# Local attention layers: outputs ahead of the query turn, MLP steps and output products one tile earlier

## The chip, the cores and the metric

The kernel runs on one core of one Trainium2 chip. The metric is device time in microseconds of one execution; the runs below are executions of the same program. The engines are named as in the profile: PE (TensorE, with PEld for its weight loads), DVE (VectorE), ACT (ScalarE), POOL (GpSimd) and SP (SyncE, whose queue issues most DMAs).

## The reference

The whole program is two adaptive layer-norm blocks over x of 4 x 1024 x 128 in float32. Block 0 is a linear attention and a mixture of experts. Block 1 is a windowed attention and, as its second half, two **local layers**. Only the local layers are touched. Cut to what matters, with 8 heads of 64 and a window of 64:

```python
def layer(x, wqkv, qs, ksc, wo, lg, lb, w1, b1, w2, b2):
    h = shift_token(x)                        # second half of the features from one token before
    q, k, v = split_heads(h @ wqkv)
    q, k = rotary_xpos(l2norm(q) * qs, l2norm(k) * ksc)
    sim = 8.0 * q @ look_around(k).T          # own window of 64 tokens and the one before, masked
    o = softmax(sim) @ look_around(v)
    x = x + merge_heads(o) @ wo
    h = layernorm(shift_token(x)) * lg + lb
    a, g = split(h @ w1 + b1)                 # 341 wide each
    return x + (a * gelu(g)) @ w2 + b2
```

## The kernel before

One function, `adaln_blocks`, builds the whole program. PE runs its instructions in the order in which the calls are written (its part is under a manual schedule). The order on DVE, ACT, POOL and SP is worked out when the program is built, by a planner that starts from the written order and lets an instruction that it takes to be ready go ahead of one that it takes to wait; a few calls are pinned with `issue_after`. Every engine then runs its own list strictly in order and waits on semaphores.

The local layers start at about 571 us. They work on tiles of 128 tokens: 8 tiles (`NT`) to a batch row, 4 rows (`B`), 2 layers (`DEPTH`), so 64 tiles. One loop over g, from -1 to 67, is a software pipeline. In round g it does, for the tiles that exist:

- `scores(g)`: 16 products of query and key (`s`, L958, 64 x 64 pieces of the array), and behind them on DVE eight masked sums with running minimum (`pr<-s`, L968, which also give `mx`).
- `project(g + 3, 0)` and `(g + 3, 1)`: the query and the key product (`qk`, L658). ACT squares each (`sq`, L661). DVE makes `co` (L663), `si` (L668) and the sum of squares `ss` (L670), in this order; `co` waits for the square. POOL adds `co` and `si` (L678), takes the power of `ss` (L674) and scales the keys (L680).
- `turn(g + 2, 0)`: four transposes of the query (`qktr`, L894), copied by ACT to `qT` (L901). For tiles 3 to 7 of the first row `co` and `si` are turned separately and added in PSUM (L898).
- `flip(g - 2, 0)` and `(g - 2, 1)`: transposes of the weights (`ptr`, L1002), copied by ACT to `pt` (L1004).
- `over_sums(g - 1)`: reciprocal (L988) and the scaling of the weights, half on POOL and half on DVE (L995); in the first row's later tiles ACT takes DVE's half (L993).
- `exps(g)`: eight exponentials on ACT (L980).
- `outputs(g - 3)`: 16 products of values and weights (`o`, L1016, 128 x 64 pieces), copied by ACT to `os` (L1020).
- `turn_keys(g + 2)`: DVE transposes the keys in blocks (`tk`, L921); SP writes them to DRAM (`kd`) and reads them back (`kT`), which `scores` needs two rounds later.
- `values(g - 1)`: the value product (`v`, L938), ACT's copy `vs` (L940) and two DMAs on SP (`ve`).
- every fourth round `project_out` (`yp`, L1027), which DVE adds to the residual (L1028).
- the side steps of a batch row, one half of 512 tokens at a time, from a table `steps`: `mlp_in` (transposes L1048, then statistics on DVE and POOL), `mlp_out` (transposes L160, ACT's `hn` L161), `mlp_gate` (L1062, then gelu on ACT, L1066, between two table loads, since exp and gelu need different tables), `mlp_up` (L1071, DVE L1073), `mlp_down` (L1079, DVE L1080) and, in the last layer, `write` (transposes L1089, ACT's copy L1091 and a DMA on SP).

All PE results but the scores go through one ring of six PSUM buffers (`pM`, tag `mid`); a new one can be written when the engines have read the one six allocations earlier. The scores have two buffers of their own (`pS`). The last batch row of the last layer has its own list of steps at the end (`parts`).

The written order of one round before was: scores, project 0, (early query turn), flip 0, over_sums, project 1, flip 1, exps, (late query turn), outputs, turn_keys, first side step, values, project_out, other side steps. The query turn stood early only in rounds 1 to 5:

```python
            if 0 < g < NT - 2:
                when(g + 2, turn, 0)
```

Of the kernel before, what the change touches and what calls it, by code (L numbers as in the profile page):

```python
# [27 lines left out]
B, N, D = 4, 1024, 128  # L28
NT = N // P
BLK = 512  # L30
# [18 lines left out]
def adaln_blocks(ctx: ExitStack, tc: tile.TileContext, a: dict, out: bass.AP):  # L49
# [637 lines left out]
    EARLY = 3  # L687
# [3 lines left out]
    with (  # L691
# [95 lines left out]
        def project_out(b, k):  # L787
            s = slice(k * BLK, (k + 1) * BLK)
            yp = ps.tile([P, BLK], F32, tag="m", name=f"y1_{b}_{k}")
            pe.matmul(yp, lhsT=wout1, rhs=kept1[b, k, "os"], start=True, stop=True)  # L790
            dve.scalar_tensor_tensor(xT[b][:, s], yp, mods[1][:, 2, b : b + 1], xT[b][:, s], ALU.mult, ALU.add)
# [23 lines left out]
        def when(g, f, *args):  # L815
            if 0 <= g < NG8:
                f(*divmod(g, NT), *args)
# [27 lines left out]
        for g in range(-1, NG8 + 2):  # L845
            b, t = divmod(g, NT)
# [30 lines left out]
    with (  # L877
# [219 lines left out]
        def at(g, f, *args):  # L1097
            steps.setdefault(g, []).append((f, args))
# [5 lines left out]
        for l in range(DEPTH):  # L1104
            for b in range(B):
                g = (l * B + b) * NT
                if (l, b) not in hs:
                    at(g - 5, shift, l, b)
                if l == DEPTH - 1 and b == last:
                    continue  # L1110
                for k, f, after in (
                    (0, mlp_in, 9), (0, mlp_out, 11), (0, mlp_gate, 12), (0, mlp_up, 13), (1, mlp_in, 13), (0, mlp_down, 14),
                    (1, mlp_out, 15), (1, mlp_gate, 16), (1, mlp_up, 17), (1, mlp_down, 18),
                ):
                    at(g + after, f, l, b, k * BLK, (k + 1) * BLK)
                if l == DEPTH - 1:
                    at(g + 16, write, l, b, 0, BLK)
                    at(g + 19, write, l, b, BLK, N)
        tiles = DEPTH * B * NT

        parts = ((0, BLK), (BLK, BLK + 2 * P), (BLK + 2 * P, N))
# [18 lines left out]
        for g in range(-1, tiles + 4):  # L1140
            side = steps.get(g, [])
            when(g, scores)
            when(g + 3, project_mid, 0)

            turns = {-1: (0, 1), 0: (2,)}.get(g, (g + 2,))
            if 0 < g < NT - 2:
                when(g + 2, turn, 0)
            when(g - 2, flip, 0)
            when(g - 1, over_sums)
            when(g + 3, project_mid, 1)  # L1150
            when(g - 2, flip, 1)
            when(g, exps)
            for i in turns:
                if not 0 < g < NT - 2:
                    when(i, turn, 0)
                if i < EARLY and g < EARLY:
                    when(i, turn, 1)
            when(g - 3, outputs)
            if g > 0:
                when(g + 2, turn_keys)  # L1160
            for f, args in side[:1]:
                f(*args)

            for i in {0: (), 1: (0,)}.get(g, (g - 1,)):
                when(i, values)

            f0 = g - 7
            if f0 % 4 == 0 and 0 <= f0 < tiles - NT:
                lo = f0 % NT * P
                project_out(f0 // (B * NT), f0 // NT % B, lo, lo + BLK)  # L1170
            for f, args in side[1:]:
                f(*args)
# [127 lines left out]
```

## Time and profile before

| | us |
|---|---|
| median of 3 runs | 1219.28 (1216.90 to 1220.04) |
| the profiled execution | 1217.85 |
| its span | 1216.0 |
| PE busy | 1117.8 |
| DVE busy | 893.6 |
| ACT busy | 799.8 |
| POOL busy | 797.0 |
| stretch 560 to 1216 (local layers), PE / DVE / ACT / POOL busy | 629.23 / 579.40 / 511.33 / 551.31 |

The span is what the profile covers; the execution's time has a little more around it. Times in views of the profile count from the start of the span. In a timeline a row gives start, duration, engine, line, operation, the tiles written and read, and in brackets the idle time of the engine just before and what ended it. Rows overlap where an engine is pipelined, so the distance from start to start says what an instruction costs in a row of others. PE's granted clock is 1.00 in almost the whole stretch.

### The profile page before, as it was taken

Reading aid. Unit: us, or ns where it says so; the run is one execution under the profiler, and the core shown is the slowest. Engines: PE = TensorE matmul, PEld = TensorE weight load, DVE = VectorE, ACT = ScalarE, POOL = GpSimd, SP = SyncE. Lnnn points to the kernel's source line nnn. Section 1 sums busy time; section 2 is a strip of 40 time slices with the busy share of each in tenths; the row PEclk is TensorE's granted clock in tenths of the full one; section 3 lists DMA queues with packets and bytes.
Section 4 is the critical chain, followed back from the end, with each engine's and each line's share of the span. In section 5 each row is a group of like instructions: output and inputs, shape, how many; then the busy total and the mean of one; then the engine's idle time right before and its main releaser. Section 6 shows DMA issues by size and latency. Waiting matters only on the chain.

```text
span 1216.0 us, 33934 instructions
## 1 busy us (share of the span) xinstructions
PE 1117.8 (92%) x13142; PEld 677.8 (56%) x13142; DVE 893.6 (73%) x2702; ACT 799.8 (66%) x2189; POOL 797.0 (66%) x712
## 2 busy tenths in 40 slices
PE   6789998999888999978899999999999999999998
PEld 5544453444366666655665555555655556555564
DVE  5557273442475577756989999999999999999854
ACT  3353372232476677755798877878878888788772
POOL 4536454747422062516899999899998999888821
PEclk9799999999999899989999999999999999999999
DMA  6030403022132132210234333343333333333320
GB/s 183 1 125 17 140 1 119 23 66 75 28 91 74 53 101 73 68 44 23 75 114 115 100 101 92 88 111 112 106 93 87 106 109 105 110 94 99 104 59 26
DMA packets 111700, 100.68 MB, mean 83 GB/s; under 512 B 9482, under 2 KB 84788, under 8 KB 111540
## 3 DMA queue, kind: packets, MB, share of 16 engines
q1 hardware_dynamic: 111108, 98.00, 27.9%
q8 instruction: 103, 1.69, 0.6%
q10 hardware_dynamic: 432, 0.53, 0.1%
q14 instruction: 57, 0.47, 0.1%
HBM read 57.71 MB, written 20.86 MB: 65 GB/s over the span
## 4 chain that ended last, share of the span: by engine, by line
PE 43%; DVE 26%; ACT 16%; issue 6%; POOL 6%; DMA 2%; SPq 2%; POOLq 0%; ACTq 0%
PE h L496 5%; DVE pr L968 4%; ACT pr L980 4%; PE ptr L751 3%; PE qk L658 3%; DVE si L668 3%; DVE ss L670 3%; DVE tk L921 2%; DVE co L663 2%; PE yp L1027 2%; PE s L958 2%; PE s L269 2%; PE obank L768 2%; PE y L510 2%; PE gm L1062 2%
## 5 line engine op out<-in xcount | busy, mean ns | idle before, releaser
L980 ACT ACTIVATE pr<-pr,mx 128x128 f32<-128x128 f32 x512 | 200.5, 403 | 51.2 <-DVE mx L968 50.5
L678 POOL TENSOR_TENSOR co<-co,si 128x512 f32<-128x512 f32 x123 | 157.7, 1285 | 68.7 <-DVE si L668 67.4
L674 POOL TENSOR_TENSOR ss<-ss,nhalf 128x16 f32<-128x16 f32 x64 | 194.6, 3041 | 5.2
L968 DVE CUSTOM_DVE_ANT_0 pr<-s,masks,ss 128x128 f32<-128x128 f32 x512 | 144.2, 345 | 12.9 <-PE s L958 12.9
L658 PE MATMUL qk<-wqkv,hs 128*128 128x512 f32 x256 | 140.4, 631 | 4.5 <-ACT pt L753 4.5
L500 POOL TENSOR_TENSOR u<-u,cw 128x512 f32<-128x512 f32 x64 | 82.0, 1283 | 81.7 <-ACT u L498 81.7
L496 PE MATMUL h<-hT,w 128*128 128x512 f32 x256 | 122.9, 603 | 6.0 <-DVE g L502 6.0
L502 DVE TENSOR_TENSOR g<-u,h 128x512 f32<-128x512 f32 x64 | 43.9, 686 | 109.1 <-POOL u L500 109.1
L498 ACT ACTIVATE u<-h 128x512 f32<-128x512 f32 x64 | 38.2, 597 | 123.2 <-PE h L496 113.9
L663 DVE TENSOR_TENSOR co<-qk,ab 128x512 f32<-128x512 f32 x128 | 86.6, 676 | 36.1 <-ACT sq L661 36.1
L290 DVE TENSOR_REDUCE mx<-s 128x8 f32<-128x896 f32 x64 | 66.8, 1086 | 51.8 <-PE s L279 51.8
L661 ACT ACTIVATE sq<-qk 128x512 f32<-128x512 f32 x128 | 75.3, 588 | 44.4 <-PE qk L658 44.1
L980 ACT ACTIVATION_READ_ACCUMULATOR pr<-pr,mx 128x1 f32 x512 | 102.1, 199 | 0.0
L1002 PEld LDWEIGHTS ptr<-ident,pr 128*128 128x128 f32 x512 | 63.4, 141 | 63.4 <-issue 50.9
L995 POOL TENSOR_TENSOR pr<-pr,sm 128x512 f32<-128x512 f32 x64 | 78.7, 1229 | 14.2 <-DVE sm L988 7.9
L668 DVE TENSOR_TENSOR si<-qk,ab 128x512 f32<-128x512 f32 x128 | 87.1, 681 | 0.0
L496 PEld LDWEIGHTS h<-hT,w 128*128 128x128 f32 x256 | 47.7, 193 | 69.9 <-issue 50.5
L670 DVE TENSOR_REDUCE ss<-sq 128x8 f32<-128x512 f32 x128 | 86.4, 675 | 0.0
L958 PEld LDWEIGHTS s<-kT,qT 64*64 64x64 f32 x2048 | 56.4, 134 | 43.6 <-issue 24.3
L958 PE MATMUL s<-kT,qT 64*64 64x128 f32 x2048 | 72.3, 278 | 7.1 <-DMA kT<-kd 6.4
L1002 PE MATMUL ptr<-ident,pr 128*128 128x128 f32 x512 | 76.4, 273 | 0.8 <-POOL pr L995 0.7
L753 ACT COPY pt<-ptr 112x512 f32<-112x512 f32 x128 | 71.6, 612 | 8.1 <-PE ptr L751 8.0
(217 smaller groups left out, 2747.9 us busy)
## 6 DMA issues: line engine op xcount, KB each, us to landing
kT<-kd SPq DMA_DIRECT2D x53, 384.0 KB, 3.5
cw<-cd SPq DMA_DIRECT2D x128, 128.0 KB, 3.0
kd<-tk SPq DMA_DIRECT2D x61, 256.0 KB, 2.4
ve<-vs SPq DMA_DIRECT2D x120, 128.0 KB, 2.3
vb<-dv SPq DMA_DIRECT2D x32, 216.0 KB, 2.8
hs<-hT SPq DMA_DIRECT2D x16, 256.0 KB, 3.8
dv<-vt SPq DMA_DIRECT2D x32, 72.0 KB, 1.6
kT<-kd SPq DMA_DIRECT2D x8, 256.0 KB, 2.7
```

The costliest lines, as they stand in the source:

```text
L496: pe.matmul(hh[:, i], lhsT=w[:, c * P : (c + 1) * P], rhs=hT[b][:, blk(k)], start=True, stop=True)
L500: pool.tensor_tensor(u, u, kept[b, k, "cw"][:, c, :], ALU.mult)
L658: pe.matmul(ps, lhsT=hs[l, b][:, t * P : (t + 1) * P], rhs=wl[l][0][:, w, :], start=True, stop=True)
L663: dve.tensor_tensor(co, ph, abs_[l][:, 0, t, w, :].unsqueeze(1).to_broadcast([P, HEADS, DH]), ALU.mult)
L668: dve.tensor_tensor(si.rearrange("p h (i e) -> p h i e", i=2), ex, sn, ALU.mult)
L670: late["summed"] = dve.tensor_reduce(ss[:, w, :], sq, AX.X, ALU.add)
L674: pool.tensor_tensor(ss, ss, nhalf[:, 0:2].unsqueeze(2).to_broadcast([P, 2, HEADS]), ALU.pow)
L678: pool.tensor_tensor(co, co, si, ALU.add)
L958: pe.matmul(S[j][qs, c, :].rearrange("p (g i) -> p g i", i=32), lhsT=q[rw, c, qs], rhs=k[rw, 2 * e : 2 * e + 4, c, :], start=True, stop=True,)
L968: dve.tensor_tensor_reduce(out=pr[:, c, :], in0=S[j][:, c, :], in1=mk[:, min(t, 1), :], scale=kept[l, b, t, "ss"][:, 0, h : h + 1], scalar ...
L980: act.activation(pr[:, c, :], pr[:, c, :], AF.Exp, bias=mx[:, j, c : c + 1], scale=-1.0, accum_out=sm[:, j, c : c + 1])
L1002: pe.transpose(tp[:, c, :], pr[:, c, :], ident)
```

## The change

Four edits in the loop of the local layers:

1. `outputs(g - 3)` stands directly behind `scores(g)`, no longer behind `exps(g)`.
2. The query turn of tile g + 2 stands behind the outputs and ahead of the first projection in all rounds with g > 0. Rounds -1 and 0 keep theirs at the old, late place.
3. All MLP steps and the writes from the table `steps` come one round earlier. The list `parts` of the last row is unchanged.
4. `project_out` comes one round earlier (g - 6 instead of g - 7).

```diff
                 for k, f, after in (
-                    (0, mlp_in, 9), (0, mlp_out, 11), (0, mlp_gate, 12), (0, mlp_up, 13), (1, mlp_in, 13), (0, mlp_down, 14),
-                    (1, mlp_out, 15), (1, mlp_gate, 16), (1, mlp_up, 17), (1, mlp_down, 18),
+                    (0, mlp_in, 8), (0, mlp_out, 10), (0, mlp_gate, 11), (0, mlp_up, 12), (1, mlp_in, 12), (0, mlp_down, 13),
+                    (1, mlp_out, 14), (1, mlp_gate, 15), (1, mlp_up, 16), (1, mlp_down, 17),
                 ):
                     at(g + after, f, l, b, k * BLK, (k + 1) * BLK)
                 if l == DEPTH - 1:
-                    at(g + 16, write, l, b, 0, BLK)
-                    at(g + 19, write, l, b, BLK, N)
+                    at(g + 15, write, l, b, 0, BLK)
+                    at(g + 18, write, l, b, BLK, N)
...
             when(g, scores)
+            when(g - 3, outputs)
+            if g > 0:
+                when(g + 2, turn, 0)
             when(g + 3, project_mid, 0)
-
-            turns = {-1: (0, 1), 0: (2,)}.get(g, (g + 2,))
-            if 0 < g < NT - 2:
-                when(g + 2, turn, 0)
             when(g - 2, flip, 0)
             when(g - 1, over_sums)
             when(g + 3, project_mid, 1)
             when(g - 2, flip, 1)
             when(g, exps)
-            for i in turns:
-                if not 0 < g < NT - 2:
-                    when(i, turn, 0)
-                if i < EARLY and g < EARLY:
-                    when(i, turn, 1)
-            when(g - 3, outputs)
+            for i in {-1: (0, 1), 0: (2,)}.get(g, ()):
+                when(i, turn, 0)
+                when(i, turn, 1)
             if g > 0:
                 when(g + 2, turn_keys)
...
-            f0 = g - 7
+            f0 = g - 6
             if f0 % 4 == 0 and 0 <= f0 < tiles - NT:
```

## The prediction

> **What bounds the kernel now.** I read the page first, then the waits, the busy time by stretches, and last the timelines of VectorE (DVE) and ScalarE (ACT) in one stretch. The page:
>
> ```profile
> PE 1117.8 (92%) x13142; PEld 677.8 (56%) x13142; DVE 893.6 (73%) x2702; ACT 799.8 (66%) x2189; POOL 797.0 (66%) x712
> PE 43%; DVE 26%; ACT 16%; issue 6%; POOL 6%; DMA 2%; SPq 2%; POOLq 0%; ACTq 0%
> ```
>
> PE looks like the bound, but the chain goes through three engines. The edit touches only the local layers, from 571 us to the end. There PE starts `s L958` once a round, and from g = 12 (671.24 us) to g = 60 (1137.92 us) the rounds repeat in fours: a gate round (`gm L1062`), an up round (`a L1071`, then `in_m L1048`), a down round (`ym L1079`) and a product round (`out_m L160`, `yp L1027`). Three such fours, s to s of the gate rounds:
>
> ```profile
> 866.72:905.06 38.34, 37.88 (x367) 22.36 (x366) 35.95 (x120) 31.32 (x98) 35.35 (x29) 1.00 0.40 108
> 905.06:943.37 38.31, 37.89 (x368) 22.36 (x367) 35.76 (x119) 31.34 (x98) 35.07 (x28) 1.00 0.32 93
> 943.37:981.76 38.39, 37.88 (x367) 22.33 (x367) 35.97 (x121) 31.33 (x98) 35.39 (x29) 1.00 0.40 108
> ```
>
> The columns are time, then busy PE, PEld, DVE, ACT, POOL. A four takes 38.3 us; DVE is idle 2.4 us in it, and nearly all of that lies in the up round:
>
> ```profile
> 915.19 0.35 DVE L968 CUSTOM_DVE_ANT_0 pr<-s,masks,ss 128x128 f32<-128x128 f32 x1 [1.29 <-PE s L958]
> ...
> 918.67 0.69 DVE L663 TENSOR_TENSOR co<-qk,ab 128x512 f32<-128x512 f32 x1 [1.23 <-ACT sq L661]
> ```
>
> `co` (and with it the whole query and key work of that round) waits for ACT's square, and ACT is late for it because of the two table loads around the gelus of the round before:
>
> ```profile
> 911.68 0.57 ACT L901 COPY qT<-qktr 128x512 f32<-128x512 f32 x1
> 912.14 0.59 ACT L1020 COPY os<-o 128x512 f32<-128x512 f32 x1
> 912.75 1.28 ACT L1066 ACT_TABLE_LOAD   x1
> 914.05 1.83 ACT L1066 ACTIVATE ge<-gm,cols 128x512 f32<-128x512 f32 x3
> 915.77 0.58 ACT L940 COPY vs<-v 128x512 f32<-128x512 f32 x1
> 916.37 1.28 ACT L980 ACT_TABLE_LOAD   x1
> 917.66 0.40 ACT L980 ACTIVATE pr<-pr,mx 128x128 f32<-128x128 f32 x1
> ...
> 918.07 0.58 ACT L661 ACTIVATE sq<-qk 128x512 f32<-128x512 f32 x1
> ```
>
> So a four is a loop over two engines. From DVE's first `pr` of the gate round (906.22) ACT takes 12.45 us to let `co` of the up round go (918.67); from there DVE runs 25.95 us without a gap over 0.15 to the first `pr` of the next gate round (944.62). Sum 38.40: the measured 38.3. PE keeps step with that loop, with stalls of its own:
>
> ```profile
> 923.29 0.27 PE L1048 MATMUL in_m<-ident,hT 64*128 64x64 f32 x1 [0.21 <-ACT qT L901]
> 923.77 0.46 PE L1048 MATMUL in_m<-ident,hT 64*128 64x64 f32 x7 [0.21 <-ACT os L1020]
> ```
>
> **The change, part by part.** No instruction is added or taken away; ACT has 27 table loads in these layers both times.
>
> *The order on ACT.* In the built program ACT's row from the gate round to the first square of the up round (e exp, s square, p `pt`, Q `qT`, O `os`, G gelu, v `vs`, L load) was `e e s p e s p e e e e e e Q O L G G G v L e s` and is now `e e O Q e s p e s p e e e e L G G G v L e O Q s`, in all twelve fours. Start to start, from the rows at 906 to 918 us: first `pr` to first exp 0.45, exp 0.39, square 0.48, `pt` 0.46, Q 0.46, O 0.47 (0.61 before a load), load 1.30, three gelus 1.72, `vs` 0.60, second load 1.29, square to `co` 0.60. Before: 0.45 + 8x0.39 + 2x0.48 + 2x0.46 + 0.46 + 0.61 = 6.52 to the load, + 4.91 to the exp, + 0.41 + 0.60 = 12.44. After: 0.45 + 3.12 + 0.96 + 0.92 + 0.46 + 0.47 = 6.38, + 4.91 + 0.41 + **0.47 + 0.46** + 0.60 = 13.23. The copies of the up round, which stood behind its squares, now stand ahead of them, and `co` comes 0.78 later. DVE's order back to the gate round is the same but for one pair, so 25.95 stays: the four becomes 39.2, and 12 x 0.78 = **+9.4**. Ends: 0.4 a four (some of it caught up in the down and product rounds) to 1.2 (every round's `co` pays): +5 to +14.
>
> *The order on PE.* In a four PE saves its `in_m` stalls: v to `in_m` 1.24 against 0.86 unstalled, `in_m` to s 0.87 against 0.48, so 0.8; each of `in_m`'s two buffers (a ring of six) will have been freed by a `qk1` and a `ptr1` instead of the late Q and O. It also changes array shape less often. Shown: s to a full product 0.10 (qk 0.96 against 0.86), transposes to o 0.09, o to a product 0.10, o to transposes 0.06. The first two go, the third becomes the fourth; s straight to o is not in the trace: 0 (both narrow) to 0.20 (leaving s and entering o in full). I take 0.10, as one switch of the nearest rows: 0.13 less a round, 0.5 a four (0.1 to 0.9). PE would need 38.3 - 0.8 - 0.5 = 37.0. That is under 39.2, so nothing of it reaches the end; PE waits for ring buffers instead. The Trainium skill ("TensorEngine Tiling (Array Packing)", Key Properties) says that changing the tiling mode drains the engine, which speaks against the end at 0; it gives no price.
>
> *DVE in the other rounds.* `qk` of the first half now ends 1.6 us later after s (product 1.08, transposes 0.5), so in the gate round `co` stands 1.0 behind the last `pr`. DVE then leaves that round 8.6 + 2.17 = 10.8 us after its start, still ahead of the 13.23: hidden, and it costs in full only if ACT's path shrinks. In the down and product rounds DVE lags by 2 to 3 us (4.0 us of `ge`, `st`, `mv`, `xh`), and the square is there first.
>
> *Head, g = 0 to 11.* In g = 3 to 5 outputs (1.1) and 16 split turns (1.8) stand ahead of `qk`: `co` can start 5.8 us after s (1.0 + 1.2 + 1.8 + 0.9 for `qk`, 0.3 to land, 0.6 square), where it stood at 5.3, 3.9 and 3.8 (598.77, 606.87, 615.25 less s); the second `co` stood at 7.7, 6.6, 6.7 and comes at 7.6. So `tk`, and the two DMAs to s two rounds later, come about 1 us later in two rounds: +1, as the chain spans two. In g = 6 to 8 `co` idles 0.6 to 1.0 behind exps and O, Q, less what DVE idled there already (0.4, 1.3, 0.5): +2. Together **+3**, from -2 (DVE, behind anyway in g = 8 to 12, swallows it and the earlier turns help) to +8.
>
> *MLP, products and writes one tile sooner.* Distances among the steps stay. The head does the same MLP work in 11 rounds, not 12, and the tail has one tile more: a round of DVE work there (7.6 us) against one of PE work here (s 1.1, o 1.1, turn 0.4, qk 1.7, ptr 0.9, v 0.9 = 6.1): 0 to -1.5, I take -0.7. In the tail the stall `a <- ACT pt` (2.00 us, at 1154.46) goes, but the last up round now carries query and key work and stalls about 1.8 as the others do; `ym` (2.7) and `otr` no longer cover the step from `in_m` to `out_m` of the second last part, beside which `gm <- ACT hn` waited 1.00 already: +1; the shape changes give -0.5. Tail **-0.4**, from -4 to +4. The six writes pass one `kd`/`kT` pair on SP; their issue (about 0.5 us each) is hidden while `kT` comes early (issued at 907.83, landed 3.5 later, 2.7 before its s) and costs up to 3 us without that.
>
> **Sum.** 9.4 + 3 - 0.4 = +12 on the profiled execution, 1217.85 (span 1216.0, 1.85 around it): 1229.9. That execution is 1.4 under the median of the three runs, 1219.28, so I give 1231.
>
> **Rivals.** *PE is the bound (faster).* For it: 98.8% busy in the fours, and the removed stalls are real. If the squares of the up round came by 10.8 us after the loop's start, not 13.2, the four would fall to PE's 37.0: -1.3 x 12 = -16, with head and tail about 1206. Against it: DVE's wait for `sq` lies in every four, and the row on ACT that ends it gets longer. The Trainium skill ("Perfetto Trace Analysis", Identifying the Most-Contended Engine) holds that matmul busy time is no measure and takes LDWEIGHTS busy and the other engines' occupancy: here 58% against DVE's 94%; by busy PE the sum would be 1206, by that rule no gain from PE's order.
>
> *The copies fall into ACT's idle time (no change).* ACT waits 45.7 us for `mx` between 690 and 1145 us; if O and Q slid into that in the up round too, the loop stays at 12.3 to 12.4 and only head and tail remain: 1219 to 1222. Against it: in the up round ACT has no idle time until the square.
>
> *`kT` becomes late too (slower still).* The `tk` of the down round ends at 934.88, 10.7 after its s; `tk` to `kT` landed is 6.5 us (904.87 to 911.3), so `kT` is there 2.0 before the s at 943.37. With DVE's later up round `tk` ends 2 later, and the two rounds take 1 more: 1.0 is left. If DMA takes that too, 0.5 to 1 us a four more: 1237 to 1243.
>
> **Chances.** Forecast 0.65, later `kT` 0.15, copies hidden 0.08, PE-bound 0.12. A run can tell 0.3%, about 3.7 us, from no change: faster 0.12, same 0.08, slower 0.80. The ends of the forecast's three terms, added in squares, are 8 us: 1223 to 1239. To leave out no more than 2 in 10, the range goes down to 1210 (the copies' case and the edge of the PE case) and up to 1242.
>
> **What would show it.** Right: fours of 39.2 us; in the up round `qT` and `os` between the second load and the square, `co <- ACT sq` at some 2.5 us there and about 1 us in the gate round; no `in_m <- ACT qT`; PE's share below 98% with new waits on DVE. Wrong: fours under 38.3, or `co` without a wait in the up round; s waiting for `kT` after g = 12 would be the third rival.

## Result and profile after

The changed kernel's median is **1232.56 us** (1229.55 to 1234.34, 4 runs) against 1218.09 us before (1216.57 to 1220.04, 4 runs): ratio 1.0125, 95% interval 1.0091 to 1.0159. It is slower, by 14.5 us; the forecast was 1231, in a range of 1210 to 1242. The profiled execution took 1232.16 us with a span of 1230.4.

From the page of the kernel after, busy times and the chain that ended last:

```profile
PE 1117.4 (91%) x13142; PEld 678.3 (55%) x13142; DVE 890.9 (72%) x2702; ACT 805.3 (65%) x2189; POOL 789.8 (64%) x712
DVE 38%; PE 32%; ACT 17%; issue 5%; POOL 3%; DMA 3%; SPq 2%; ACTq 0%; POOLq 0%
```

The instruction counts are those of before. In the chain DVE and PE have changed places (before: PE 43%, DVE 26%).

Where the time went, by stretches (start:end, length, busy PE, PEld, DVE, ACT, POOL, then PE's clock, DMA share, GB/s). The cuts are the first `s` of the layers, the `s` of tile 12, that of tile 60, and the end. Before:

```profile
573.43:671.24 97.81, 90.16 (x967) 58.85 (x967) 92.29 (x318) 81.73 (x290) 87.72 (x74) 0.97 0.34 97
671.24:1137.92 466.68, 458.77 (x4421) 270.52 (x4420) 436.33 (x1444) 378.81 (x1181) 428.18 (x343) 1.00 0.35 100
1137.92:1216.00 78.08, 69.78 (x589) 43.47 (x588) 42.72 (x154) 44.44 (x120) 25.16 (x24) 1.00 0.21 60
```

After:

```profile
573.37:673.42 100.05, 90.89 (x973) 60.52 (x973) 91.07 (x318) 81.62 (x288) 86.62 (x73) 0.96 0.33 95
673.42:1150.73 477.31, 455.89 (x4421) 266.85 (x4421) 433.23 (x1442) 382.28 (x1179) 419.49 (x342) 1.00 0.35 98
1150.73:1230.40 79.67, 68.93 (x583) 43.96 (x582) 44.20 (x158) 46.14 (x126) 26.52 (x27) 0.97 0.20 57
```

Head +2.2, the twelve fours +10.6, tail +1.6. In the fours PE's busy time fell by 2.9 us and the stretch still grew.

The same place as before, one four in DVE's timeline (four rows; the first and third are the first `pr` of the gate round and of the up round):

```profile
906.10 0.36 DVE L968 CUSTOM_DVE_ANT_0 pr<-s,masks,ss 128x128 f32<-128x128 f32 x1
...
909.30 0.69 DVE L663 TENSOR_TENSOR co<-qk,ab 128x512 f32<-128x512 f32 x1 [0.94 <-ACT sq L661]
...
914.76 0.34 DVE L968 CUSTOM_DVE_ANT_0 pr<-s,masks,ss 128x128 f32<-128x128 f32 x1
...
919.56 0.69 DVE L663 TENSOR_TENSOR co<-qk,ab 128x512 f32<-128x512 f32 x1 [2.54 <-ACT sq L661]
```

From 906.10 to 919.56 is 13.46 us, the ACT part of the loop; it was 12.45. Before, the wait for `s` in the up round (1.29) and that for the square (1.23) stood one behind the other; now `s` is there in time and the whole 2.54 is a wait for the square. ACT's timeline shows what holds it:

```profile
906.56 0.40 ACT L980 ACTIVATE pr<-pr,mx 128x128 f32<-128x128 f32 x1 [2.77 <-DVE mx L968]
...
912.14 0.41 ACT L980 ACTIVATE pr<-pr,mx 128x128 f32<-128x128 f32 x1
...
912.66 1.28 ACT L1066 ACT_TABLE_LOAD   x1
913.95 1.83 ACT L1066 ACTIVATE ge<-gm,cols 128x512 f32<-128x512 f32 x3
915.68 0.58 ACT L940 COPY vs<-v 128x512 f32<-128x512 f32 x1
916.28 1.28 ACT L980 ACT_TABLE_LOAD   x1
917.57 0.40 ACT L980 ACTIVATE pr<-pr,mx 128x128 f32<-128x128 f32 x1
...
917.97 0.56 ACT L1020 COPY os<-o 128x512 f32<-128x512 f32 x1
918.44 0.58 ACT L901 COPY qT<-qktr 128x512 f32<-128x512 f32 x1
918.92 0.61 ACT L661 ACTIVATE sq<-qk 128x512 f32<-128x512 f32 x1
```

The first row closes the loop: ACT's exponentials of the gate round wait for DVE's minimum `mx`, which the first `pr` gives. Between the exponential at 917.57 and the square at 918.92 stand the two copies, 0.95 us; before, the square followed the exponential directly. PE now waits for ACT's late copies in its ring, instead of the `in_m` stalls of before:

```profile
918.59 2.84 PE L1071 MATMUL a<-hn,w 128*128 128x512 f32 x6 [1.04 <-ACT os L1020]
...
922.69 0.46 PE L1048 MATMUL in_m<-ident,hT 64*128 64x64 f32 x7 [0.19 <-DVE si L668]
```

### The profile page after: what moved, and what is told of

The parts are those of the page before. It is cut to its first block, busy times and chain, and to the rows that moved or that the text cites. A ratio compares the mean times of both kernels' runs of the same rounds, so it can differ in the third digit from the quotient of the medians.

```text
span 1230.4 us, 33903 instructions
## 1 busy us (share of the span) xinstructions
PE 1117.4 (91%) x13142; PEld 678.3 (55%) x13142; DVE 890.9 (72%) x2702; ACT 805.3 (65%) x2189; POOL 789.8 (64%) x712
## 4 chain that ended last, share of the span: by engine, by line
DVE 38%; PE 32%; ACT 17%; issue 5%; POOL 3%; DMA 3%; SPq 2%; ACTq 0%; POOLq 0%
DVE pr L968 5%; PE h L496 5%; DVE tk L921 5%; DVE ss L670 5%; DVE si L668 5%; DVE co L663 4%; ACT pr L980 3%; PE ptr L751 3%; DVE pr L995 3%; ACT sq L661 2%; PE s L269 2%; PE y L510 2%; PE obank L768 2%; POOL u L500 2%; DVE ge L1073 2%
## 5 line engine op out<-in xcount | busy, mean ns | idle before, releaser
L674 POOL TENSOR_TENSOR ss<-ss,nhalf 128x16 f32<-128x16 f32 x64 | 187.6, 2932 | 5.2
L658 PE MATMUL qk<-wqkv,hs 128*128 128x512 f32 x256 | 132.4, 600 | 6.1 <-ACT pt L753 4.2
L980 ACT ACTIVATION_READ_ACCUMULATOR pr<-pr,mx 128x1 f32 x512 | 104.7, 204 | 0.0
```

The lines of the kernel that those rows point to most:

```text
L658: pe.matmul(ps, lhsT=hs[l, b][:, t * P : (t + 1) * P], rhs=wl[l][0][:, w, :], start=True, stop=True)
L674: pool.tensor_tensor(ss, ss, nhalf[:, 0:2].unsqueeze(2).to_broadcast([P, 2, HEADS]), ALU.pow)
L980: act.activation(pr[:, c, :], pr[:, c, :], AF.Exp, bias=mx[:, j, c : c + 1], scale=-1.0, accum_out=sm[:, j, c : c + 1])
```

## The experiments

**Theory:** in the fours the time is a loop of an ACT part (first `pr` of the gate round to the first `co` of the up round) and a DVE part (from there to the next gate round's first `pr`), and the change lengthens the first by the two copies. The two parts add up to the four by definition. What speaks for a loop is that the DVE part holds hardly a wait: in the kernel after, DVE waits 24 times between 690 and 1130 us, 40.2 us in all, each time for a square, and 22 of these are in gate and up rounds, ahead of the DVE part. **Rivals:** PE's new order does it (the projection comes later behind outputs and turn), or the earlier MLP steps and products do.

The table gives the ratio to the kernel before with its interval (as on record, against runs of the kernel before taken in the same set, whose medians lay between 1218.08 and 1220.17 us, so it is not the quotient of two rows), the ACT part, the DVE part and the four (each the mean of four consecutive fours of the profiled execution, from rows as above; in `shift` three of the four are 40.5 to 40.8 us and one is 42.2) and the local layers (first `s` to the end of the span). The last is the steadier measure for small differences: the start of the local layers, behind source that is the same in all, lay between 569.3 and 579.2 us in these profiled executions.

| kernel | median us | ratio (95%) | ACT part | DVE part | four | local layers |
|---|---|---|---|---|---|---|
| before | 1218.09 | | 12.45 | 25.89 | 38.34 | 642.6 |
| after | 1232.56 | 1.0125 (1.0091-1.0159) | 13.45 | 25.89 | 39.33 | 657.0 |
| outs | 1230.72 | 1.0090 (1.0057-1.0124) | 12.93 | 25.91 | 38.84 | 649.7 |
| turn | 1225.30 | 1.0051 (1.0025-1.0078) | 12.93 | 25.88 | 38.80 | 649.9 |
| orders | 1233.79 | 1.0135 (1.0105-1.0165) | 13.42 | 25.79 | 39.21 | 655.5 |
| shift | 1253.70 | 1.0272 (1.0233-1.0311) | 12.52 | 28.48 | 41.01 | 673.8 |
| shift_prod | 1220.36 | 1.0025 (1.0006-1.0044) | 12.44 | 26.36 | 38.81 | 645.7 |
| outs_shift | 1224.01 | 1.0050 (1.0022-1.0078) | 12.93 | 26.00 | 38.93 | 650.7 |
| behind | 1221.38 | 1.0021 (1.0001-1.0041) | 12.45 | 26.03 | 38.48 | 646.1 |
| up_old | 1222.52 | 1.0008 (0.9985-1.0031) | 12.52 | 26.05 | 38.57 | 646.2 |
| sq_first | 1214.00 | 0.9944 (0.9913-0.9975) | 11.62 | 26.06 | 37.68 | 637.3 |
| sq_first_before | 1215.80 | 0.9965 (0.9941-0.9989) | 11.14 | 27.02 | 38.16 | 639.8 |
| best | 1201.70 | 0.9843 (0.9812-0.9874) | 10.80 | 26.04 | 36.84 | 626.9 |
| best_late | 1207.00 | 0.9896 (0.9866-0.9927) | 10.81 | 25.94 | 36.75 | 628.2 |

### The edits one by one

`outs`, edit 1 alone on the kernel before:

```diff
             when(g, scores)
+            when(g - 3, outputs)
             when(g + 3, project_mid, 0)
...
-            when(g - 3, outputs)
```

> Edit 1 alone. Loop theory (the four is the ACT part from DVE's first pr of the gate round to co of the up round, 12.45 us before and 13.44 after, plus 25.9 us of DVE): only os stands ahead of the square, so the ACT part is 12.9, the four 38.8, 12 x 0.47 = +5.6, about 1224 (1221 to 1227). Rival, PE order (qk comes later behind work that PE does first; o takes 1.08 us and the turn 0.49): the 14 us split by these, +9.5, about 1228. Rival, shift (the earlier MLP steps cost it): no change.

`turn`, edit 2 alone:

```diff
             when(g, scores)
+            if g > 0:
+                when(g + 2, turn, 0)
             when(g + 3, project_mid, 0)
...
-            for i in turns:
-                if not 0 < g < NT - 2:
-                    when(i, turn, 0)
...
```

> Edit 2 alone. Loop theory: only qT stands ahead of the square, ACT part 12.9, four 38.8, +5.6, about 1224 (1221 to 1227): the same as for the outputs alone, although PE's part is less than half as long. Rival, PE order: +4.5, about 1222.5, with the square ended by PE's qk. Rival, shift: no change.

Both have an ACT part of 12.93 and a four of 38.8, as the loop theory said, although the outputs take PE more than twice as long as the turn; the local layers grew by 7.1 and 7.3 us. So PE's time does not count here; the number of copies ahead of the square does. The median of `outs` lies above its 1221 to 1227, and its six runs reach from 1225.98 to 1235.57. Its local layers do not show that: its profiled execution begins them 5.7 us later than before. Why, stays open.

`orders`, edits 1 and 2:

> Edits 1 and 2, steps and products at their old rounds. Theory: fours as in the changed kernel, ACT part 13.44, DVE part 25.9, four 39.3; 12 x 0.95 = +11.4 and head +2: 1229 to 1233; what is left to the changed kernel (the tail) is within 2 us.

Four 39.21, local layers +12.9 of the change's +14.4 (the median, 1233.79, is a little over the 1233 of the expectation): edits 1 and 2 carry the loss.

### Edits 3 and 4

`shift`, the tables of steps and `f0 = g - 6` of the change, the loop's order as before:

> Edits 3 and 4 alone. Loop theory: ACT's order in the fours is that of before, ACT part 12.45, fours 38.3 to 38.4; head and tail alone move, by -2 to +3: 1216 to 1221. Rival, shift: +8 or more.

This was wrong by over 30 us, and not in the ACT part. The waits of PE in 690 to 1140 us (engine, line, releaser: total, times, longest), and a row of DVE's timeline:

```profile
PE yp L1027 <- ACT os L1020: 20.6, 11, 2.1
```

```profile
911.03 0.69 DVE L1028 TENSOR_TENSOR hT<-hT,yp 128x512 f32<-128x512 f32 x1 [1.64 <-PE yp L1027]
```

With g - 6, the product `yp` reads the `os` of `outputs(g - 3)`, copied in the same round; with the outputs late, PE and then DVE stand and wait (2.1 us at most, 11 times on PE). The expectation had looked at the order around the square alone. `shift_prod` tests that cause: edits 3 and 4, and the outputs early in the product rounds alone.

```diff
+            if g % 4 == 2:
+                when(g - 3, outputs)
             when(g + 3, project_mid, 0)
...
-            when(g - 3, outputs)
+            if g % 4 != 2:
+                when(g - 3, outputs)
```

> Edits 3 and 4, with the outputs early in the product rounds alone. Edits 3 and 4 by themselves gave fours of 40.5 us, 28.1 in the DVE part. Theory: only because yp then reads the os that is copied in the same round, late. With that os early the wait is gone, nothing stands ahead of the squares of the up rounds, ACT part 12.45, fours 38.3 to 38.5: 1216 to 1221. Rival (the steps' new place costs it): 1245 or more stays.

The local layers come back from 673.8 to 645.7. The fours stay 0.3 to 0.5 above the expected 38.3 to 38.5, in the DVE part; that rest was not followed up. `outs_shift` is edits 1, 3 and 4:

> Edits 1, 3 and 4, the turn late. Theory: edits 3 and 4 are free once the outputs are early: fours as with edit 1 alone, ACT part 12.93, four 38.8 to 38.9; head and tail +1 to +3; 1223 to 1228. Rival: over 1235.

Four 38.93 against 38.84 without the shift, local layers 650.7 against 649.7: once the outputs are early, edits 3 and 4 move nothing much either way.

### Undoing the copies' place

`behind` has the whole change and its order on PE; only ACT's two copies of the up round are issued behind the second square, with the later exponentials behind that square too. `outputs` and `turn` only note their copies down, and `copies()` issues them:

```diff
+            up = 12 <= g < 61 and g % 4 == 0
...
+            if not up:
+                copies()
             when(g + 3, project_mid, 0)
...
             when(g + 3, project_mid, 1)
+            if up:
+                with tc.issue_after(late["squared"].ins):
+                    copies()
             when(g - 2, flip, 1)
-            when(g, exps)
+            when(g, exps, *((1,) if up else ()))
```

> The whole change, PE's written order untouched, but in the 13 up rounds ACT copies os and qT behind the second square, as before. Loop theory: ACT part back to 12.5, fours 38.4 to 38.5, 12 x 0.95 = 11 under the changed kernel, about 1221 (1218 to 1224). Rival, PE order: PE is unchanged, so 1232 stays. What the copies' later end does to PE's ring of buffers (a behind o) is not counted: at most 0.5 us a four.

ACT's timeline of `behind` in one up round (L890 are both copies, L987 the exponentials):

```profile
914.48 1.28 ACT L987 ACT_TABLE_LOAD   x1
915.77 0.40 ACT L987 ACTIVATE pr<-pr,mx 128x128 f32<-128x128 f32 x1
916.17 0.57 ACT L661 ACTIVATE sq<-qk 128x512 f32<-128x512 f32 x1
...
917.61 0.59 ACT L890 COPY os<-o 128x512 f32<-128x512 f32 x1
918.07 0.61 ACT L890 COPY qT<-qktr 128x512 f32<-128x512 f32 x1
```

The square follows the exponential again, the ACT part is 12.45, and of the 14.4 us in the local layers 10.9 are back, with PE's order untouched. The four is 38.48, so PE's new order, which stands here in all rounds, brings nothing against the 38.34 of before. `up_old` puts turn and outputs of the up rounds back on PE as well:

> The whole change, but in the up rounds PE does turn and outputs at the late place of before, with ACT's copies there too. Loop theory: ACT part 12.5, fours 38.4, about 1221 (1218 to 1224), as where only the copies are put behind. If PE's order counts by itself: lower than that run by over 3 us.

646.2 against 646.1 us in the local layers: PE's order in the up rounds adds nothing while this loop sets the time. Most of the 3.5 us that stay in `behind` is there at tile 12 already (+3.3, counted from the first `s`): the head, where nothing was put back.

### Shortening the loop

If the ACT part sets the four, taking the second table load out of it must gain, whatever PE's order is. `sq_first` is the changed kernel with the exponentials of the up round behind the squares, so that the square needs no wait for the load:

```diff
-            when(g, exps)
+            if 12 <= g < 61 and g % 4 == 0:
+                with tc.issue_after(late["squared"].ins):
+                    when(g, exps)
+            else:
+                when(g, exps)
```

> The whole change, but the eight exponentials of the up round stand behind its two squares on ACT, so that the squares run ahead of the second table load (the square needs no load of its own); os and qT still ahead of the squares. Loop theory: the ACT part loses the load, 1.29, and an exponential, 0.40: 11.75, four 37.65, 12 x 1.7 to 1.9 = 20 to 23 under the changed kernel: about 1211 (1207 to 1216). Rival, PE order: no change from 1232.

The ACT part fell from 13.45 to 11.62 and the four from 39.33 to 37.68, as the loop theory said; the median, 1214.00, is in its band, and PE's order was not touched.

`sq_first_before` is the same move on the kernel before, in its up rounds:

> The kernel before with the same move of the squares ahead of the second load. Loop theory: ACT part 10.75, DVE's loop 36.7; now PE's 37.9 a four bounds: -0.4 to -0.5 a four, about 1212.5 (1209 to 1216). If the loop over ACT and DVE does not set the four: no change, 1218.

Its four is 38.16, not 37.9. Busy times of one of its fours, and the row of DVE in the up round:

```profile
907.59:945.75 38.16, 37.81 (x367) 22.36 (x368) 35.83 (x120) 31.47 (x98) 33.84 (x29) 1.00 0.32 94
```

```profile
916.56 0.35 DVE L968 CUSTOM_DVE_ANT_0 pr<-s,masks,ss 128x128 f32<-128x128 f32 x1 [1.27 <-PE s L958]
```

DVE no longer waits for the square there; it waits for PE's `s`. PE is busy for 37.81 of the 38.16 us, so with the old order the bound is now PE with its stalls, and the shorter ACT part brought only 0.2 of its 1.3 us. `best` is the changed kernel with squares, then copies, then load and exponentials (as `behind`, with all eight exponentials held back):

```diff
-            when(g, exps, *((1,) if up else ()))
+            when(g, exps, *((0,) if up else ()))
```

> The whole change, with the squares of the up round first on ACT (ahead of os, qT and the second load). Loop theory: ACT part 10.8, DVE's loop 36.7, PE's own 37.0 a four then bounds, where its new order's saved stalls count: 37.1 a four, 12 x 2.4 = 29 under the changed kernel, about 1203 (1198 to 1212; the upper end if a waits for the later os in the ring, up to 0.8 us a four). If PE's order saves nothing: as for the kernel before with the squares first, 1212.5.

A four of it, and ACT's up round (with the added lines L1073 is the gelu, L946 the copy `vs`, L987 the load for the exponentials):

```profile
898.10:934.80 36.70, 36.70 (x369) 21.95 (x368) 35.70 (x120) 31.57 (x98) 34.44 (x29) 1.00 0.34 99
```

```profile
906.11 1.83 ACT L1073 ACTIVATE ge<-gm,cols 128x512 f32<-128x512 f32 x3
907.83 0.58 ACT L946 COPY vs<-v 128x512 f32<-128x512 f32 x1
908.29 0.61 ACT L661 ACTIVATE sq<-qk 128x512 f32<-128x512 f32 x1
...
909.87 0.58 ACT L890 COPY os<-o 128x512 f32<-128x512 f32 x1
910.34 0.60 ACT L890 COPY qT<-qktr 128x512 f32<-128x512 f32 x1
...
911.45 1.28 ACT L987 ACT_TABLE_LOAD   x1
```

PE is busy without a break and DVE 97%. 1201.70 us beats both kernels: the one before by 1.6% (1.3 to 1.9), and the changed one's median of 1232.56, from another set of runs, by 30.9 us (30.1 in the local layers). Against before, the stretch from tile 12 to tile 60 is 18.7 us shorter (448.0 against 466.7) and the tail 2.8, but the head is 5.8 longer (103.7 against 97.8). Of PE's 1.3 us a four between `sq_first_before` and `best`, 0.6 is the stall within `in_m`: from its start to `s` 1.01 us there (924.38 to 925.39), 0.40 here (913.18 to 913.58). How the rest divides among the changes of array shape was not tested. `best_late` drops edits 3 and 4 from it:

> As the kernel with the squares of the up round first and os, qT behind them, but with steps and products at their old rounds. Theory: PE's saving comes from edits 1 and 2, fours of 36.7 to 37.1, 1200 to 1205. Rival (PE's saving needs edits 3 and 4): fours of 37.9 or more, 1212 or more.

Its fours are those of `best` (36.75 against 36.84) and its local layers 1.3 us longer: PE's saving comes from edits 1 and 2. Its median of 1207 is 2 us above its band, and the two ratios' intervals meet at 0.987; whether edits 3 and 4 are worth something more here is not settled.

## Why the prediction was right, and where it was off

**The main term** was the right mechanism, at the place named, with the waits that it named: 2.54 us for the square in the up round (some 2.5 forecast), 0.94 in the gate round (about 1). `behind` shows that the order of two copies on ACT carries it, `outs` and `turn` that each copy costs its own 0.48. The size was 0.78 a four; the ACT part grew by 1.00 (12.45 to 13.45). The term that was mis-sized is the 6.38 us to the first load: it is 6.56 in the rows. Eight exponentials were put at 0.39, 3.12 together; they took 3.28, most of it in the last, which stands 0.52 ahead of the load (912.14 to 912.66). The 0.14 that the prediction took off with `os` (0.61 ahead of a load, 0.47 elsewhere) belongs to whatever stands there, and nothing is saved. (In the prediction's row of ACT before there is one `e` too many; its sum counts the eight that the trace has.) The DVE part stayed at 25.89, as assumed. Twelve fours from gate round to gate round grew by 11.6 us (466.6 before, 478.2 after). The change's gate rounds come one tile earlier, so the stretch between the same two tiles shows +10.6 for the +9.4 forecast.

**Head:** +2.2 for +3. **Tail:** +1.6 for -0.4. The tail's `a <- ACT pt` of 2.00 went as said, and a wait came for `kT` of the last tile, as in the third rival, but in a single place:

```profile
1176.72 1.22 PE L958 MATMUL s<-kT,qT 64*64 64x128 f32 x32 [2.74 <-DMA kT<-kd]
```

**The number** was in part luck. The forecast change was +11.7 (1231 less 1219.28), the measured one +14.5: the fours and the tail were put too low, by 1.2 and 2.0, the head too high by 0.8. That 1231 came within 1.6 us of 1232.56 is helped by the 1.2 us by which the median before came out lower, at 1218.09.

**PE's saving** was forecast at 1.3 a four and as useless under the loop. Both hold: the four of `behind`, with that order, is no shorter than before, and once the ACT part is at 10.8, the condition that the first rival named, the four is 36.84 (37.0 forecast) against PE's 38.16 in the old order. The price of `s` straight to `o`, taken at 0.10 between 0 and 0.20, is about 0.04: the first group of `o` behind `s` takes 0.16 us to the next (903.78 to 903.94), the following ones 0.12. The Trainium skill ("TensorEngine Tiling (Array Packing)", Key Properties) speaks of a drain at such a change. Here the change costs these 0.04 us; whether a drain is what takes them, the rows do not show.

**Wrong in a detail:** PE's new waits were said to be on DVE. They are mostly on ACT: `a <- ACT os`, 1.04 in the four shown.

**The rivals.** PE as the bound: refuted by the fours of 39.33 us in which PE is busy for less than before. Copies hidden in ACT's idle time: refuted by the rows at 917.97 and 918.44. `kT` late in the fours: no; between 690 and 1140 us three waits, 2.3 us in all.

## What to carry to other kernels

Before an instruction is moved on one engine, read where its consumers land in the other engines' queues: here 1.6 us of work on PE moved, and what counted were two copies of 0.48 us each that came ahead of one square on ACT. Where two engines hand a loop back and forth, look for that loop before counting on savings of a third: here PE's 1.3 us a four were worth nothing until the loop was shorter, and then nearly all of it. The same edits cost 14 us of the local layers with the copies ahead of the squares and took part in a gain of 16 with the squares first. An edit that lets a consumer come a round earlier must be read together with the one that makes its producer earlier; alone it cost 31 us.

## What the runs showed of the hardware

- A square ran behind a gelu without a table load of its own: in `best` it follows `ge` and `vs` at 908.29, and the number of loads (14 and 13 in these layers) did not change. So in this kernel the squares can stand on either side of the load.
- A table load here costs its 1.28 us and about 0.13 in the instruction ahead of it (0.52 in place of 0.39 for an exponential, start to start). `sq_first` took a load and an exponential out of the ACT part, which fell by 1.83: less the 0.40 of the exponential, the switch is worth 1.43. The Trainium skill ("ScalarE: Activation LUTs", What ACT_TABLE_LOAD costs) has 2.66 us for a switch, load and drain together; here only about half of that stands in the way of the next instruction, and the measurement decides.
